# The product of the weights moved ahead of the branch, and the last rows of a two-layer graph kernel rearranged

## The chip, the core and the metric

One core of a Trainium2 chip runs the whole program. Its engines are TensorE (PE, matrix products), VectorE (DVE), ScalarE (ACT), GpSimd (POOL) and SyncE (SP, which here only issues DMAs); ACT and POOL issue DMAs too. The metric is the device time of one execution, in microseconds; less is better. All data are float32.

## What is computed

32 batches of 512 rows by 512 features pass through two graph layers, each with a layer norm ahead of it and the input added behind it:

```
h = max(layernorm(x), 0)
x = x + (adj @ h) @ weight + bias                    # layer 0
h = max(layernorm(x), 0)
q, k, v = h @ Wq + bq, h @ Wk + bk, h @ Wv + bv      # layer 1, 8 heads
scores = q k^T / sqrt(64) + (1 - adj) * -1e9
x = x + (softmax(scores) v) @ Wo + bo
```

`adj` is a 512 by 512 matrix shared by all batches, with values under 1, so in layer 1 the factor -1e9 leaves for each row one neighbour, the one with the largest value, unless two of them are close. The attention then only picks a row of `h`, and layer 1 becomes `h[largest neighbour] @ (Wv Wo) + (bv Wo + bo)`.

## The kernel before

**Ahead of the branch** (lines 68 to 176, `gnn_two_layers`). The kernel loads adj and x of batch 0 in four chunks of 128 rows each, on SP's and ACT's queues, transposes adj on TensorE into `adjT`, normalizes batch 0 into `hs[0]`, and computes that batch's first aggregate, `yT` = (adj h) transposed (line 139, 16 products of 128 by 512, two passes each). Beside it DVE makes the mask (line 115), finds each row's largest neighbour (`top`, `sel`, `idx`), counts the rows that are anyone's neighbour (`used`, line 148, from the small products `few`), and decides whether the shortcut is safe (lines 154 to 167, from `many`); the norms of Wq and Wk enter through ACT's squares. The answer is `flag`, one number that every engine loads (line 178). Then the program branches into `single_path` (taken here, with room for 336 distinct neighbours) or into the general attention.

**Behind the branch** (`single_path`). Each batch needs three large products: `aggregate` (adj h), `layer0` (times the weight) and `layer1` (times `wvo` = Wv Wo, on the rows that are anyone's neighbour only). `product` (line 288) does each in seven pieces on half-size blocks instead of eight, with sums of blocks made by DVE beforehand (`sum_a`, `sum_b`: `h0s`, `adjT_s`, `w0_t`, `yTs` in `sel`, `hTs`, `wvo_t`). Pieces p1, p5, u2, c11, c22, c12, c21 run in that order over three PSUM banks; c22, c12 and c21 add onto a bank that holds an earlier piece, so that piece must first be taken out by `take` (DVE adds or ACT copies). In the last batch's layer0 (line 457) c22 stands ahead of c11.

**The order of the work** is written out by hand. A round `b` has 21 steps, each the length of one piece: steps 0 to 6 under `layer0(b)`, 7 to 13 under `aggregate(b + 1)`, 14 to 20 under `layer1(b - 1)`. `put(batch, step, f)` hangs the work of the other engines on a step; `run` (line 573) emits a piece's products, then the functions of the step, then the piece's take. Each engine runs its own instructions in the order in which they are emitted, so whatever is emitted first also stands first in that engine's queue. Round 0 runs `layer0_rows(0)` and `aggregate(1)`, and in place of a layer 1 `fold_weights` (line 366): it transposes Wv and multiplies it with Wo into `wvo`, and makes `cvo` and `cvo_c`, the bias row and column, from bv, Wo and bo. The loads of Wv and Wo into `xs[3]` and `xs[4]` are the first DMAs behind the branch (line 595). `number_rows` (line 408) gives each used row its place, ten small operations on DVE with two tiny products.

**Rows travel through DRAM.** `put_h` scatters a batch's `h` with indirect DMAs on POOL, so that used rows stand together; `get_h` reads them back (`hc`), `transpose_h` turns them (`hT`); `layer1` writes `zs` (`take_z`); `put_z` transposes and stores it as `z`; `finish` gathers each row's result from `z` by `place` and adds it to `x`; `store` writes the batch out. `look_up` (line 427) fills `place` with four small gathers on POOL, once, in round 1. `zs` has one buffer; its last columns are set to zero by a POOL memset (line 536) that is emitted where `layer1` begins.

**The end.** The last batch, 31, takes its rows by gather from `hs` into `hs[0]` (`get_all`), transposes them (`transpose_all`) and multiplies row chunk by row chunk (`layer1_rows`, line 508). Batches 29 and 30 get their `z` by plain gathers (`fetch`) into `late_z`, and DVE adds them (`add_z`) between the row chunks of batch 31, each followed by its store.

Of the kernel before, what the change touches and what calls it, by code (L numbers as in the profile page):

```python
# [8 lines left out]
F32 = mybir.dt.float32  # L9
# [8 lines left out]
P = 128  # L18
# [7 lines left out]
def gnn_two_layers(ctx: ExitStack, tc: tile.TileContext, x, adj, w0, b0, wq, bq, wk, bk, wv, bv, wo, bo, out):  # L26
# [22 lines left out]
    def big(name):  # L49
# [3 lines left out]
    adjT, yT, w0_s, sel = big("adjT"), big("yT"), big("w0_s"), big("sel")  # L53
    wv_s, wo_s = xs[3], xs[4]
    b0_r = keep.tile([P, D], F32, name="b0_r")
# [7 lines left out]
    kept = dict(xs=xs, hs=hs, adjT=adjT, yT=yT, w0_s=w0_s, sel=sel, wv_s=wv_s, wo_s=wo_s, b0_r=b0_r, used=used,  # L63
                before=before, idx=idx, ident=ident, ones=ones, mhalf=mhalf)
# [3 lines left out]
    with ExitStack() as tmp, tc.manual_schedule():  # L68
# [3 lines left out]
        mask = look.tile([P, C, N], F32, name="mask")  # L72
        for c in range(C):
            nc.sync.dma_start(mask[:, c, :], adj[c * P:(c + 1) * P, :])
            nc.scalar.dma_start(xs[0][:, c, :], x[0, c * P:(c + 1) * P, :])
# [3 lines left out]
        wt = [look.tile([P, DC, D], F32, name=f"wt{i}") for i in range(2)]  # L79
        bt = [look.tile([P, DC], F32, name=f"bt{i}") for i in range(2)]  # L80

        def load_w(t, w):
            nc.scalar.dma_start(t, w.rearrange("(c p) o -> p c o", p=P))

        norms = [Norm(nc, small, mhalf, xs[0], hs[0], [0, 1]), Norm(nc, small, mhalf, xs[0], hs[0], [2, 3])]
        pts = [ps_l.tile([P, C, P], F32, name=f"pt{m}") for m in range(C)]
        for c in range(C):
            for m in range(C):
                nc.tensor.transpose(pts[m][:, c, :], mask[:, c, m * P:(m + 1) * P], ident)
            norms[c // 2].stats(c % 2)  # L90
            if c == 1:
                norms[0].power()
            if c == 2:
                norms[0].offset()
        norms[1].power()
        for t, v in zip(bt, (bq, bk)):
            nc.gpsimd.dma_start(t, v.rearrange("(c p) -> p c", p=P))
        nc.gpsimd.dma_start(b0_r, bass.AP(tensor=b0.tensor, offset=b0.offset, ap=[[0, P], [1, D]]))
        for i, w in enumerate((wq, wk)):
            norms[0].relu(i)  # L100
            load_w(wt[i], w)
        for m in range(C):
            eng = (nc.scalar.copy, nc.scalar.copy, nc.vector.tensor_copy, nc.vector.tensor_copy)[m]
            eng(adjT[:, m, :], pts[m].rearrange("p c q -> p (c q)"))
        norms[1].offset()
        for i in range(2):
            norms[1].relu(i)
        if B > 1:
            load_w(xs[1], x[1])
        load_w(w0_s, w0)  # L110

        sums = look.tile([P, 4], F32, name="sums")
        top = look.tile([P, C, 8], F32, name="top")
        for c in range(C):
            nc.vector.tensor_scalar(mask[:, c, :], mask[:, c, :], 1.0, NEG, op0=ALU.subtract, op1=ALU.mult)
            nc.vector.max(top[:, c, :], mask[:, c, :])
            nc.vector.tensor_scalar(sel[:, c, :], mask[:, c, :], top[:, c, 0:1], None, op0=ALU.is_equal)
        both = look.tile([P, N], F32, name="both")
# [6 lines left out]
        nc.vector.tensor_reduce(least, gap, AX.X, ALU.min)  # L125

        if B > 1:
            norms.append(Norm(nc, small, mhalf, xs[1], hs[1], range(C)))
            norms[2].stats(0)
            norms[2].stats(1)  # L130
        few = ps_l.tile([P, 4, C], F32, name="few")
        many = ps_l.tile([P, 4, C], F32, name="many")
        for d in range(DC):
            ps = ps_l.tile([P, N], F32, name="mm", bufs=2)
            for m in range(C):
                if d == 3 and m == 2:
                    nc.tensor.matmul(many[:, 0, :], ones, used, start=True, stop=True)
                    nc.tensor.matmul(many[:, 1, :], ones, sums, start=True, stop=True)
                nc.tensor.matmul(ps, hs[0][:, m, d * P:(d + 1) * P], adjT[:, m, :], start=(m == 0), stop=(m == C - 1))  # L139
            if d < 2:  # L140
                nc.scalar.activation(bt[d], bt[d], AF.Square, accum_out=sums[:, 2 * d + 1:2 * d + 2])
            nc.scalar.copy(yT[:, d, :], ps)
            if d < 2:
                nc.scalar.activation(wt[d], wt[d], AF.Square, accum_out=sums[:, 2 * d:2 * d + 1])
            if d == 2:
                for m in range(C):
                    nc.tensor.matmul(few[:, 0, m:m + 1], both[:, m * P:(m + 1) * P], ones[:, 0:1], start=True, stop=True)
                nc.vector.tensor_scalar_min(used, few[:, 0, :], 1.0)
                if B > 1:
                    norms[2].stats(2)  # L150
                    norms[2].stats(3)
                    norms[2].power()
        rows = look.tile([P, 1], F32, name="rows")
        nc.vector.tensor_reduce(rows, many[:, 0, :], AX.X, ALU.add)
        fits = look.tile([P, 1], F32, name="fits")
        nc.vector.tensor_scalar(fits, rows, float(ROOM[0]), None, op0=ALU.is_le)
# [798 lines left out]
```

## Time and profile before

| what | us |
|---|---|
| median of 3 runs (lowest, highest) | 1096.13 (1095.85, 1096.92) |
| the profiled execution | 1098.71 |
| its span, first to last instruction | 1097.0 |
| ahead of the branch: first product of the aggregate (line 139) | 10.79 |
| flag written | 29.09 to 29.23 |
| first product behind the branch (line 464) | 30.34 |
| product of the weights, 32 passes (line 378) | 60.36 to 74.26 |
| first piece of layer0(1) | 74.96 |
| last product of TensorE ends | 1087.02 |

A line of the timeline reads: start, duration, engine, line, operation, written tile <- read tiles, shape, count (instructions of one kind in a row are merged), and in brackets the engine's idle time just before with what ended it. The list of waits reads: engine and line that waited <- what released it: total, times, longest. A releaser is inferred from semaphore events and can be missing ("unknown queue"). Ends of matmuls are modelled.

### The profile page before, as it was taken

The page shows a single profiled execution, that of the slowest core. Times are in us where ns is not written, and L with a number is a line of the kernel's source. Part 1 is how long each engine was busy: PE and PEld are TensorE (multiplying, and loading weights), DVE is VectorE, ACT ScalarE, POOL GpSimd, SP SyncE. Part 2 cuts the span into 40 slices and gives each one's busy share as a digit, 9 for nine tenths or more (in the row PEclk, how much of TensorE's full clock was granted, in tenths as well). Part 3 has the DMA queues.
Part 4 walks back from the last instruction along what each step waited for, and adds up shares of the span by engine and source line. Part 5 has one row for each costly group of instructions (what it writes and reads, how often), then busy time and mean ns, then how long its engine had stood idle before and what let it go on. Part 6 is the DMA issues. An engine that isn't in the chain of part 4 may idle for free.

```text
span 1097.0 us, 15882 instructions
## 1 busy us (share of the span) xinstructions
PE 1071.3 (98%) x5404; PEld 941.6 (86%) x5404; DVE 903.2 (82%) x1854; ACT 357.0 (33%) x655; POOL 445.7 (41%) x522
## 2 busy tenths in 40 slices
PE   7999999999999999999999999999999999999996
PEld 3558899999989989989998998999998899999883
DVE  6868888898888889878888888888988888898863
ACT  4223232333223233323233322323332232333221
POOL 1124443335543334544333554443355434345422
PEclk9999999999999999999999999999999999999999
DMA  7362666677676667766667767666777766676547
GB/s 239 125 142 66 156 160 155 185 198 182 180 174 153 159 187 201 180 169 159 163 167 201 184 184 172 152 171 174 202 179 183 171 147 172 183 196 152 147 118 228
DMA packets 162412, 186.90 MB, mean 170 GB/s; under 512 B 14993, under 2 KB 102289, under 8 KB 162321
## 3 DMA queue, kind: packets, MB, share of 16 engines
q1 hardware_dynamic: 130672, 112.70, 37.5%
q0 software_dynamic: 27968, 66.61, 27.0%
q10 hardware_dynamic: 3680, 6.49, 1.7%
q8 instruction: 44, 0.72, 0.3%
q14 instruction: 48, 0.39, 0.1%
HBM read 96.28 MB, written 89.46 MB: 169 GB/s over the span
## 4 chain that ended last, share of the span: by engine, by line
PE 91%; DVE 3%; DMA 2%; POOL 1%; issue 1%; ACT 1%; another core or an unknown queue 0%; SPq 0%; ACTq 0%; POOLq 0%; DVEq 0%
PE mm L294 85%; PE mm L139 2%; PE mm L464 1%; PE mm L378 1%; POOL x L552 1%; PE mm L514 1%; DMA yT<-z,place 1%; DMA x<-in_x_dram 1%; DMA z<-zr 0%; DVE st L199 0%; ACT h L217 0%; DVE zr L543 0%; DVE x L351 0%; DMA hc<-hs 0%
## 5 line engine op out<-in xcount | busy, mean ns | idle before, releaser
L552 POOL DMA_INDIRECT x<-z,place x116 | 182.8, 1576 | 366.3 <-DMA z<-zr 299.4
L333 ACT COPY yT<-mm 128x512 f32<-128x512 f32 x124 | 71.8, 579 | 561.1 <-PE mm L294 487.6
L351 DVE TENSOR_TENSOR x<-mm,x 128x512 f32<-128x512 f32 x217 | 149.7, 690 | 86.1 <-PE mm L294 86.1
L217 ACT ACTIVATE h<-x,off,rstd 128x512 f32<-128x512 f32 x256 | 194.9, 808 | 41.3 <-DVE off L209 40.5
L206 POOL TENSOR_TENSOR rstd<-ve,mhalf 128x2 f32<-128x2 f32 (+1 forms) x97 | 106.5, 1098 | 218.5 <-DVE ve L205 218.3
L199 DVE BATCH_NORM_STATS2 st<-x 128x6 f32<-128x512 f32 x256 | 171.6, 670 | 9.2 <-DMA x<-in_x_dram 8.0
L294 PE MATMUL mm<-w_t,sel 128*128 128x256 f32 x744 | 171.0, 379 | 0.8 <-DVE x L351 0.8
L294 PE MATMUL mm<-adjT_s,h0s 128*128 128x256 f32 x744 | 171.0, 379 | 0.7 <-ACT yT L333 0.7
L294 PEld LDWEIGHTS mm<-w_t,sel 128*128 128x128 f32 x744 | 141.2, 190 | 20.7 <-DVE x L351 1.6
L294 PEld LDWEIGHTS mm<-adjT_s,h0s 128*128 128x128 f32 x744 | 141.1, 190 | 20.7 <-ACT yT L333 1.6
L476 POOL DMA_INDIRECT hs<-h,dest x124 | 133.2, 1075 | 31.2 <-issue 22.2
L294 PE MATMUL mm<-adjT,h 128*128 128x256 f32 x496 | 117.2, 379 | 0.0
L294 PE MATMUL mm<-w_s,yT 128*128 128x256 f32 x496 | 117.2, 379 | 0.0
L294 PE MATMUL mm<-hTs,wvo_t 128*128 128x168 f32 x720 | 113.7, 307 | 3.5 <-ACT zs L344 3.5
L344 ACT ACTIVATE zs<-mm,cvo_c 128x168 f32<-128x168 f32 x248 | 85.6, 397 | 88.6 <-PE mm L294 84.9
L294 PEld LDWEIGHTS mm<-hTs,wvo_t 128*128 128x128 f32 x720 | 106.0, 191 | 4.2 <-ACT zs L344 4.2
L294 PEld LDWEIGHTS mm<-adjT,h 128*128 128x128 f32 x496 | 94.2, 190 | 13.2 <-issue 0.5
L294 PEld LDWEIGHTS mm<-w_s,yT 128*128 128x128 f32 x496 | 92.9, 190 | 11.7 <-issue 0.5
L442 DVE TENSOR_TENSOR x<-x,b_r 128x512 f32<-128x512 f32 x128 | 86.6, 678 | 0.0
L294 PE MATMUL mm<-hT,wvo 128*128 128x168 f32 x480 | 79.4, 309 | 0.0
L294 PEld LDWEIGHTS mm<-hT,wvo 128*128 128x128 f32 x480 | 73.8, 192 | 1.5
L331 DVE TENSOR_TENSOR yT<-mm,yT 128x512 f32<-128x512 f32 x93 | 63.9, 687 | 7.0 <-PE mm L294 3.0
(148 smaller groups left out, 1273.4 us busy)
## 6 DMA issues: line engine op xcount, KB each, us to landing
out_dram<-x SPq DMA_DIRECT2D x124, 256.0 KB
x<-in_x_dram SPq DMA_DIRECT2D x120, 256.0 KB
hc<-hs SPq DMA_DIRECT2D x124, 176.0 KB
z<-zr SPq DMA_DIRECT2D x120, 96.0 KB
z<-zr SPq DMA_DIRECT2D x120, 80.0 KB
hs<-h,dest POOLq DMA_INDIRECT x124, 6.2
x<-z,place POOLq DMA_INDIRECT x116
x<-in_x_dram ACTq DMA_DIRECT2D x4, 256.0 KB
```

The costliest lines, as they stand in the source:

```text
L139: nc.tensor.matmul(ps, hs[0][:, m, d * P:(d + 1) * P], adjT[:, m, :], start=(m == 0), stop=(m == C - 1))
L199: self.nc.vector.bn_stats(st, self.src[:, self.chunks[i], :])
L206: self.nc.gpsimd.tensor_tensor(self.rstd, ve, self.mhalf[:, 0:n], ALU.pow)
L217: self.nc.scalar.activation(dst, src, AF.Relu, bias=self.off[:, i:i + 1], scale=self.rstd[:, i:i + 1])
L294: nc.tensor.matmul(bank[:, m, 0:half], lhs[:, k, m * P:(m + 1) * P], rhs[:, k, :], start=(first and m == 0 and k == 0), stop=(k == 1), ski ...
L331: nc.vector.tensor_add(dst, bank, dst)
L333: nc.scalar.copy(dst, bank)
L344: nc.scalar.activation(dst[:, m, :], bank[:, m, :], AF.Identity, bias=cvo_c[:, 2 * i + m:2 * i + m + 1])
L351: nc.vector.tensor_add(dst, bank, dst)
L442: nc.vector.tensor_add(X[b][:, c, :], X[b][:, c, :], b0_r)
L476: stored = nc.gpsimd.indirect_dma_start(out=HS[b], out_offset=bass.IndirectOffsetOnAxis(ap=dest[:, i:i + 1], axis=0), in_=H1[b][:, i, :], ...
L552: nc.gpsimd.indirect_dma_start(out=X[b][:, c, :], out_offset=None, in_=Z[b], in_offset=bass.IndirectOffsetOnAxis(ap=place[:, c:c + 1], axi ...
```

## The change

Two ends of the program change; rounds 2 to 28 keep their code.

Front: Wv and Wo are loaded first, chunk by chunk on both queues, then adj, x of batch 0, Wq, Wk, w0 and x of batch 1, all on SP. Wv is transposed and multiplied with Wo ahead of the branch; adj is transposed between the four parts of that product, by which ACT instead of DVE makes the mask, in two operations for each chunk. Then comes the aggregate of batch 0. The product for `flag` stands two products ahead of the aggregate's end, the counts a chunk earlier. `cvo`, `cvo_c`, the sums of adjT and the first two of w0, and the addition of b0 to batch 0 are done ahead of the branch. Behind it, `number_rows` moves to step 1, some norms, sums and scatters of round 0 to earlier steps, `look_up` from step 11 to step 16 of round 1; round 0 has no third product any more.

End: the last batch's layer0 has the order of pieces of the others; batch 30's `zs` takes the buffer of `h0s`; two stores of batch 29's `z` go to ACT's queue; the first `transpose_all` is at step 18 of round 31; the row chunk's own addition and store come ahead of the `add_z`, which are spread two to each chunk.

The diff, cut to its core:

```diff
+    adjT, yT, w0_s, sel, wvo = big("adjT"), big("yT"), big("w0_s"), big("sel"), big("wvo")
+    adjT_s, w0_t = (keep.tile([P, 4, 2, N // 2], F32, name=n) for n in ("adjT_s", "w0_t"))
     wv_s, wo_s = xs[3], xs[4]
...
+        wt = [look.tile([P, DC, D], F32, name=f"wt{i}") for i in range(2)]
+        bt = [look.tile([P, DC], F32, name=f"bt{i}") for i in range(2)]
+        bv_c = look.tile([P, DC], F32, name="bv_c")
+        wvT = yT
...
+        for t, w in ((wv_s, wv), (wo_s, wo)):
+            for c in range(DC):
+                (nc.sync, nc.scalar)[c % 2].dma_start(t[:, c:c + 1, :], rows(w, c, 1))
+        for t, w in ((adj_s, adj), (xs[0], x[0])):
+            for c in (0, 2):
+                nc.sync.dma_start(t[:, c:c + 2, :], rows(w, c, 2))
+        for t, w in [(wt[0], wq), (wt[1], wk), (w0_s, w0)] + [(xs[1], x[1])] * (B > 1):
+            nc.sync.dma_start(t, rows(w, 0, C))
         make_identity(nc, ident)
         nc.gpsimd.memset(ones, 1.0)
         nc.gpsimd.memset(mhalf, -0.5)
...
+        for t, v in ((bv_c, bv), (bt[0], bq), (bt[1], bk)):
+            nc.gpsimd.dma_start(t, v.rearrange("(c p) -> p c", p=P))
+        first = look.tile([P, 1], F32, name="first")
+        nc.scalar.activation(first, ones[:, 0:1], AF.Relu)
...
+        for _ in transposed(wv_s, wvT, (nc.scalar.copy, nc.vector.tensor_copy, nc.scalar.copy, nc.vector.tensor_copy)):
+            pass
+        for c in range(C):
+            nc.scalar.activation(mask[:, c, :], adj_s[:, c, :], AF.Copy, bias=-1.0)
+            nc.scalar.activation(mask[:, c, :], mask[:, c, :], AF.Copy, scale=NEG)
...
+        flips = transposed(adj_s, adjT, (nc.scalar.copy,) * 4)
+        for i in range(DC):
+            ps = ps_l.tile([P, D], F32, name="mm", bufs=2)
+            for j in range(DC):
+                nc.tensor.matmul(ps, wvT[:, j, i * P:(i + 1) * P], wo_s[:, j, :], start=(j == 0), stop=(j == DC - 1))
+            if i == 0:
+                next(flips)
+                peaks(0)
+                peaks(1)
+            if i == 1:
+                next(flips)
+                for n in (0, 1):
+                    norms[0].stats(n)
+                norms[0].power()
+                for v, r in ((b0, b0_r), (bo, cvo)):
+                    nc.gpsimd.dma_start(r, bass.AP(tensor=v.tensor, offset=v.offset, ap=[[0, P], [1, D]]))
+                norms[1].stats(0)
+                norms[0].offset()
+                norms[1].stats(1)
+                norms[1].power()
+            nc.scalar.copy(wvo[:, i, :].rearrange("p (c q e) -> p q c e", q=4, c=4),
+                           ps.rearrange("p (q c e) -> p q c e", q=4, c=4))
+            if i == 1:
+                next(flips)
+                norms[0].relu(0)
+                norms[0].relu(1)
+                peaks(2)
+                norms[1].offset()
...
+        for i in range(4):
+            sum_b(nc, adjT_s, adjT, i)
...
         for d in range(DC):
             ps = ps_l.tile([P, N], F32, name="mm", bufs=2)
             for m in range(C):
-                if d == 3 and m == 2:
+                if d == 2 and m == 1:
                     nc.tensor.matmul(many[:, 0, :], ones, used, start=True, stop=True)
                     nc.tensor.matmul(many[:, 1, :], ones, sums, start=True, stop=True)
+                if d == 3 and m == 2:
+                    nc.tensor.matmul(few[0:1, 1, 0:1], sure, ones[:, 0:1], start=True, stop=True)
+                if d == 3 and m == 0:
+                    bias = ps_l.tile([P, D], F32, name="pt0")
+                    nc.tensor.matmul(bias, ones, part, start=True, stop=True)
                 nc.tensor.matmul(ps, hs[0][:, m, d * P:(d + 1) * P], adjT[:, m, :], start=(m == 0), stop=(m == C - 1))
-            if d < 2:
...
-            if d == 2:
+            if d == 0:
+                squares(1)
                 for m in range(C):
                     nc.tensor.matmul(few[:, 0, m:m + 1], both[:, m * P:(m + 1) * P], ones[:, 0:1], start=True, stop=True)
...
+                for i in range(2):
+                    sum_b(nc, w0_t, w0_s, i)
+                if B > 1:
+                    norms[2].offset()
+            if d == 2:
+                decide()
+                nc.vector.memset(before[:, 0:1], 0.0)
+                for m in range(1, C + 1):
+                    nc.vector.tensor_add(before[:, m:m + 1], before[:, m - 1:m], many[:, 0, m - 1:m])
+                for c in (0, 1):
+                    nc.vector.max_index(idx[:, c, :], top[:, c, :], mask[:, c, :])
         nc.vector.tensor_copy(flag, few[0:1, 1, 0:1])
+        for c in (2, 3):
+            nc.vector.max_index(idx[:, c, :], top[:, c, :], mask[:, c, :])
+        nc.vector.tensor_add(cvo, bias, cvo)
+        nc.vector.tensor_mul(part.rearrange("p (c q e) -> p c q e", q=4, c=4),
+                             cvo.rearrange("p (q c e) -> p c q e", q=4, c=4),
+                             ident.rearrange("p (q e) -> p q e", q=4).unsqueeze(1).broadcast_to([P, 4, 4, 32]))
+        nc.vector.tensor_reduce(cvo_c, part.rearrange("p (c n) -> p c n", c=DC), AX.X, ALU.add)
         if B > 1:
-            norms[2].offset()
             for c in range(C):
                 norms[2].relu(c)
-        nc.vector.memset(before[:, 0:1], 0.0)
-        for m in range(1, C + 1):
-            nc.vector.tensor_add(before[:, m:m + 1], before[:, m - 1:m], many[:, 0, m - 1:m])
-        for c in range(C):
-            nc.vector.max_index(idx[:, c, :], top[:, c, :], mask[:, c, :])
+        for c in range(C):
+            nc.vector.tensor_add(xs[0][:, c, :], xs[0][:, c, :], b0_r)
 
...
     def layer0(b):
-        if b == B - 1:
-            return product(yT, yTs, w0_s, w0_t, take_onto(X[b]), pieces=("p1", "p5", "u2", "c22", "c11", "c12", "c21"))
...
-            for bz, c in ((), ((B - 3, 0), (B - 3, 1)), ((B - 3, 2), (B - 3, 3)), [(B - 2, c) for c in range(C)])[r]:
-                add_z(bz, c, nc.sync if bz == B - 3 else nc.scalar)
             x_r = X[b][:, r, :].rearrange("p (q c e) -> p q c e", q=4, c=4)
             nc.vector.tensor_add(x_r, bank.rearrange("p (c q e) -> p q c e", q=4, c=4), x_r)
             nc.sync.dma_start(out[b, r * P:(r + 1) * P, :], X[b][:, r, :])
+            for i in range(2):
+                add_z(B - 3 + r // 2, 2 * (r % 2) + i, nc.sync if r < 2 else nc.scalar)
...
-        ZT[b] = work.tile([P, DC, 32 * S], F32, name="zs")
+        ZT[b] = work.tile([P, DC, 32 * S], F32, name="h0s" if b == B - 2 else "zs")
...
-            eng = nc.scalar if b == B - 2 and s0 == 0 and q > 1 else nc.sync
+            eng = nc.scalar if q > 1 and (b, s0) in ((B - 3, 6), (B - 2, 0)) else nc.sync
...
-        for t, w in ((wv_s, wv), (wo_s, wo)):
-            nc.sync.dma_start(t, w.rearrange("(c p) o -> p c o", p=P))
-        nc.gpsimd.dma_start(bv_c, bv.rearrange("(c p) -> p c", p=P))
-        nc.gpsimd.dma_start(cvo, bass.AP(tensor=bo.tensor, offset=bo.offset, ap=[[0, P], [1, D]]))
...
-                put(b + 2, 2, load_x)
+                put(b + 2, 2 * b, load_x)
...
-            put(b, 9 if b > 0 else 15, put_h, 0)
...
+            put(b, 9, put_h, 0)
...
-            for step, i in ((13, 0), (13, 1), (13, 2), (14, 3)) if b == B - 2 else \
-                    ((14, 0), (15, 1), (16, 2), (18, 3)) if b > 0 else ((14, 0), (16, 1), (17, 2), (18, 3)):
+            for i, step in enumerate((13, 13, 13, 14) if b in (0, B - 2) else (14, 15, 16, 18)):
...
+            if b == 0:
+                put(0, 1, lambda b: number_rows())
+                for i in (2, 3):
+                    put(0, 12, lambda b, i: sum_b(nc, w0_t, w0_s, i), i)
...
+            if b == B - 1:
+                put(b, 18, lambda b: transpose_all(0))
...
-                put(1, 11, lambda b: look_up(tables[0]))
-                for step, i in ((4, 0), (4, 1), (5, 2), (5, 3)):
+                put(1, 16, lambda b: look_up(tables[0]))
...
-            if b == 0:
-                for step, c in ((0, 0), (0, 1), (1, 2), (2, 3)):
...
-                for step, i in ((0, 0), (0, 1), (1, 2), (1, 3)):
-                    put(0, step, lambda b, i: sum_b(adjT_s, adjT, i), i)
...
-                put(0, 11, lambda b: number_rows())
-                for step, i in ((11, 0), (12, 1), (12, 2), (13, 3)):
...
-                for j in range(DC):
-                    put(0, 16 + j, lambda b, j: bias_part(j), j)
...
             run(aggregate(b + 1) if b + 1 < B else layer1(b - 2) if b < B else None, todo[7:14])
-            if b == 0:
-                run(fold_weights(), todo[14:21])
-            else:
-                run(layer1(b - 1) if b < B and b != B - 2 else None, todo[14:21])
+            run(layer1(b - 1) if 0 < b < B and b != B - 2 else None, todo[14:21])
```

## Prediction

> **What bounds the kernel now.** I read the page first (busy shares, then the chain that ended last), then TensorE's own waits, then its timeline at the front, at 100 us and at the end, and last what DVE, ACT and POOL do in those places.
>
> ```profile
> PE 1071.3 (98%) x5404; PEld 941.6 (86%) x5404; DVE 903.2 (82%) x1854; ACT 357.0 (33%) x655; POOL 445.7 (41%) x522
> PE 91%; DVE 3%; DMA 2%; POOL 1%; issue 1%; ACT 1%; another core or an unknown queue 0%; SPq 0%; ACTq 0%; POOLq 0%; DVEq 0%
> ```
>
> TensorE is busy for 98% of the span and is 91% of the chain, nearly all of it line 294, the seven-piece products. The change leaves those products alone, so a gain can only come from time in which TensorE stands still, or runs slowly. The list of its waits is short:
>
> ```profile
> PE pt L89 <- DMA mask<-in_adj_dram: 5.2, 3, 4.8
> PE mm L294 <- ACT zs L344: 3.5, 2, 2.7
> PE mm L464 <- ACT h L217: 1.3, 1, 1.3
> PE mm L294 <- DVE yT L331: 1.1, 1, 1.1
> PE mm L139 <- ACT adjT L104: 1.1, 1, 1.1
> PE mm L294 <- issue: 0.9, 1, 0.9
> PE mm L514 <- ACT h L503: 0.8, 1, 0.8
> PE mm L294 <- DVE x L351: 0.8, 1, 0.8
> ```
>
> Its timeline says where they are: at the front, once at 101.8 us, and in the last 60 us.
>
> ```profile
> 4.76 2.27 PE L89 MATMUL pt<-ident,mask 128*128 128x128 f32 x8 [4.76 <-DMA mask<-in_adj_dram]
> 10.79 13.36 PE L139 MATMUL mm<-adjT,h 128*128 128x512 f32 x24 [1.07 <-ACT adjT L104]
> 56.22 1.99 PE L294 MATMUL mm<-adjT_s,h 128*128 128x256 f32 x8 [1.10 <-DVE yT L331]
> 60.36 13.90 PE L378 MATMUL mm<-x,zs 128*128 128x512 f32 x32
> 104.49 1.95 PE L294 MATMUL mm<-hTs,wvo_t 128*128 128x168 f32 x8 [2.67 <-ACT zs L344]
> 106.23 2.45 PE L294 MATMUL mm<-hT,wvo 128*128 128x168 f32 x8
> 1045.03 1.99 PE L294 MATMUL mm<-w_t,sel 128*128 128x256 f32 x8 [0.79 <-DVE x L351]
> 1064.43 1.41 PE L294 MATMUL mm<-adjT_s,wvo_t 128*128 128x168 f32 x8 [0.92 <-issue]
> 1071.70 1.98 PE L514 MATMUL mm<-wvo,h 128*128 128x512 f32 x4 [0.82 <-ACT h L503]
> ```
>
> See that until 10.79 us TensorE has done nothing but 16 transposes, while the product of the weights (60.36, 13.90 us) is done later, when it is the bound. Between 109 and 1013 us the table of stages shows it busy throughout but for one idle 0.7 us.
>
> **What the Trainium skill says.** "TensorE: Matmul & The Clock Gate", Part 1, says the array runs at half rate until it has been busy for a free-running window of about 3.4 us, and goes back after an idle one. The trace agrees: 24 passes took 13.36 us where 24 x 0.429 = 10.3 would do, and after the idle 2.67 us the pieces at 104 and 106 us took 1.95 and 2.45 instead of 1.30. Part 4 there says that transposes don't count as busy for this gate; the trace agrees, since after 16 transposes the products at 10.79 were still slow. "DMA: Bandwidth & Descriptors", Issuing engines are not separate DMA queues, says that loads issued by several engines share the same 16 engines; here 2 MB on two queues moved at 395 to 402 GB/s (4 to 8 us), later loads on ACT's queue alone at 228 to 408.
>
> **The change, part by part**, against the profiled execution (1098.71 us, span 1097.0; the median of the runs is 1096.13, 2.58 lower).
>
> *Front.* The wv chunks take the places of the adj and x chunks in the queues, so the first lands at about 4.8 us as these did. Sixteen transposes at 2.27/8 each end at 9.3; the first copy (0.6) is done by then since its last transpose is the first of the last four. wo's chunks follow at 7.3 to 8.7, as the later adj and x chunks did. So 32 product passes start at 9.3, not the aggregate at 10.79: -1.5. The adj transposes move into the fast stream, 16 x 0.13 = +2.1 (the weights' own run there now at 1.04 per 8); the weights' transposes leave it (58.05 to 60.36), -2.3. The slow clock is met once as before, by one stream instead of the other: 0, +-0.9 for where the window falls.
>
> What must keep up: adj (next 1 MB, at 350 GB/s by 12) is wanted at 16, x0 (by 15) at 24 by ACT's norms. ACT's list up to the aggregate is 2 copies, 8 mask operations (nearest row 0.81, about 0.7 in a chain: 5.7 us, 11.5 to 17.5), wvo copies of 0.59, 4 adjT copies after TensorE's last adj transposes (21.7 to 24), 4 norms of 0.73 with a wvo copy between, to 27.3. TensorE ends the product at 9.3 + 13.7 + 2.5 (slow clock) + 2.1 = 27.6, and wants the last chunk of h 1.7 us later. Hidden, with 2 us to spare. POOL's loads of bv, bq and bk now come first, 1.18 and 0.81 to issue as before, where POOL is idle until 7.4; at 6.9 to landing bv is there by 9, for the bias part. The early activation takes the table load (1.28, at 4.87 before) out of the way of the first copy: 0, as ACT was idle. DVE (copies, bias part 2.7, four peaks of 1.2, four norm statistics of 0.9, sums) is done by 27. The aggregate with its small products ends at 43.4.
>
> *Flag.* Before, flag was written at 29.23, after TensorE's last product, and it restarted at 30.34; idle from about 28.8, 1.5 us. Now the small product for it stands two products (four passes) before the end, so flag is written about 1.5 us before TensorE ends, and the load and branch (0.9 us) are covered. What is late next: the first bank after the branch was the bias sum's, which DVE reads after flag and two index searches (2 x 0.75): about 44.2, 0.7 to 0.8 after the end. -0.8; ends 0 and -1.2. The b0 additions (4 x 0.6) now stand on DVE ahead of the branch, and the row takes wait behind them to 48.7; six banks cover that.
>
> *First batch.* number_rows moves from step 11 to step 1: its ten small DVE operations (53.3 to 55.0) no longer delay the yT take: -1.1. Folding's bias product (2 passes) only moves. layer0(1) follows aggregate(1) directly; its sums are emitted at step 13, as for the batch 31 before, where the trace shows no gap (1037.17 to 1042). The norms of the first rounds come some steps earlier, cvo and the sums of adjT and w0 ahead of the branch, the weights' loads are gone from SP behind it, so x2 comes sooner: the same instructions beside a busy TensorE, 0. Steps 14 to 20 of the first round, spread under the folding before, now follow in one go; DVE has one yT sum (0.7) there. So layer0(1) starts at 74.96 - 1.5 - 0.2 - 0.8 - 1.1 = 71.4: **-3.6**, ends -2.3 and -4.9.
>
> *Places.* At 101.8 TensorE waits for ACT's first zs take, and ACT for something the trace calls an unknown queue, until 103.7. Just then, once in the run, POOL issues four place gathers (97.38 to 102.38) ahead of zs's memset, beside SP's hc loads. They go to step 16, behind the memset and the rstd. I take the wait as theirs: 2.67 idle, and the slow clock after it, 111.97 - 104.49 = 7.48 us for five pieces of 1.14, 1.78 lost: **-4.45**. The other end is 0: the trace doesn't show that the gathers are the cause. Behind them at step 16 POOL has only finish(0), at 119 us, with 15 us idle ahead.
>
> *End.* Plain order of pieces in the last layer0: c11 stands between u2 and c22 again, so the bank is taken in time: -1.05 (13.14 us from 1038.90 to 1052.04 against 7 x 1.726). zs of batch 30 in h0s's buffer removes ACT's wait for DVE's transposes of batch 29's zs (0.92). But two z stores of batch 29 now go out on ACT's queue, 0.85 for two, ahead of ACT's c21 take: p1's take ends about 3.1 us after the product starts, wanted at 2.3. So that stall stays: 0. First transposes of the last rows at step 18, as their gather (1062.6 + 4.6) lands: -0.82. TensorE ends 1.9 earlier. Behind it, gather and add of batch 30's z: last gather landed at 1090.5, then the row add, queued behind it on DVE, 0.6, then a store. The z stores and gathers move with TensorE by 1.05; the row add now stands ahead of the last two z adds: 1.05 + 0.6, and out stores of batch 29 start one row earlier, freeing DMA (share 1.00 at 1075 to 1080): **-2.4**, ends -1 and -3.5.
>
> Sum: -3.6 - 4.45 - 2.4 = -10.45, so 1098.71 becomes 1088.3. The profiled run lies above the others by 2.58; I do not know how much of the one-off stall the others have, so I keep 1088 as the forecast for the median too, a gain of 8.
>
> **Rivals.**
> - *The stall at 101.8 isn't the gathers'*, or is not in ordinary runs. For: the trace names no queue, memset's columns don't overlap the takes. Against: nothing else is peculiar to that place. Then 1096.13 - 6.0 = 1090.1.
> - *ACT takes over at the front.* It now has masks, copies and norms in one file; if the norms end 3.6 us after 27.6 the front's gain is gone, and the stall may stay too: about 1093.7. For: they queue behind four copies. Against: ACT is 33% busy, slack 2 us.
> - *Slower: x1 late.* All eight MB follow on SP's queue, x1 last, and DVE's statistics of x1 stand ahead of `used`, which TensorE wants at about 36 for the counts. Landing after 35 costs TensorE a us for each us, and from 43 on, a mean of 190 GB/s after the first 2 MB, more than the whole gain; at 46 us of landing, with the clock slowed again, 1099. Against: 228 to 408 GB/s puts it at 24 to 32.
>
> **How the numbers follow.** Forecast 0.45, stall stays 0.28, ACT 0.13, slower 0.14. The first two hold 1083.3 (all far ends) to 1092.8 (all near ends); with half of the third the range is 1083.3 to 1093.8. Within 0.2% (2.2 us, about what can be told from no change) falls half of the ACT case: faster 0.79, same 0.07, slower 0.14.
>
> **What would show it.** First product at about 9.3 us, layer0_rows at 44, layer0(1) at 71.4, no wait on DVE's yT; no idle TensorE at about 98, no second slow stretch of the clock; in the last 60 us the waits on DVE x and ACT h gone, the two on ACT's zs left; the last DVE operation a z add. Wrong: TensorE waiting on `used` or on h near 28 to 36 us, or a new wait within the first two batches.

## The result: 1084.9 us, and the profile after

| | before | after |
|---|---|---|
| median (lowest to highest) | 1096.53 (1095.85 to 1097.96), 4 runs | 1084.90 (1083.45 to 1085.40), 4 runs |
| ratio, 95% interval | | 0.989 (0.9873 to 0.9907) |
| the profiled execution; its span | 1098.71; 1097.0 | 1083.45; 1081.3 |
| first piece of layer0(1) | 74.96 | 67.65 |
| layer0(1) to layer0(2) | 37.01 | 33.24 |
| layer0(2) to layer0(31) | 926.93 | 926.46 |
| layer0(31) to TensorE's last product | 48.12 | 45.65 |
| from there to the end of the span | 9.97 | 8.33 |

The change gains 11.6 us; 8 was forecast, with 1083.3 to 1093.8 as the range. TensorE's list of waits in the kernel after (total, times, longest):

```profile
PE pt L106 <- DMA x<-in_L_gnn_Wv_dram: 4.7, 1, 4.7
PE mm L364 <- ACT zs L414: 1.4, 2, 0.8
PE mm L364 <- DVE zs L411: 0.8, 1, 0.8
PE mm L491 <- ACT yT L209: 0.7, 1, 0.7
PE mm L364 <- ACT yT L403: 0.3, 1, 0.3
PE mm L364 <- issue: 0.3, 1, 0.3
```

The waits on DVE's yT, on DVE's x and on ACT's h are gone; of the ones on ACT's zs, two are left where there were three (3.5 us of two and the 0.92 shown as issue). One is new, on DVE's zs. TensorE's timeline after says where:

```profile
4.66 3.57 PE L106 MATMUL pt<-ident,x 128*128 128x128 f32 x16 [4.66 <-DMA x<-in_L_gnn_Wv_dram]
8.35 3.94 PE L134 MATMUL mm<-x,yT 128*128 128x512 f32 x8
...
13.00 3.60 PE L134 MATMUL mm<-x,yT 128*128 128x512 f32 x8
...
41.31 7.11 PE L491 MATMUL mm<-w_s,yT 128*128 128x512 f32 x16 [0.72 <-ACT yT L209]
...
67.65 1.89 PE L364 MATMUL mm<-w_s,yT 128*128 128x256 f32 x8
...
99.65 1.41 PE L364 MATMUL mm<-hTs,wvo 128*128 128x168 f32 x8 [0.82 <-DVE zs L411]
...
1051.54 1.41 PE L364 MATMUL mm<-adjT_s,wvo_t 128*128 128x168 f32 x8 [0.64 <-ACT zs L414]
...
1067.68 5.32 PE L541 MATMUL mm<-wvo,h 128*128 128x512 f32 x12
```

See the first three lines. Sixteen transposes stand back to back, 0.22 us each; the eight product passes behind them take 3.94 us where eight at full rate (third line) take 3.60. So the clock is full almost from the first product; the trace's own record of the clock puts the step (the moment at which it becomes full) at 8.03 us. In the kernel before, 24 passes took 13.36 us instead of 10.3, and the step came at 16.46. Near 100 us there is no wait of 2.7 us and no second slow stretch. The last operations of DVE after:

```profile
1074.46 0.68 DVE L543 TENSOR_TENSOR x<-mm,x 128x512 f32<-128x512 f32 x1
1075.07 0.68 DVE L593 TENSOR_TENSOR x<-yT,x 128x512 f32<-128x512 f32 x1
1076.38 0.69 DVE L593 TENSOR_TENSOR x<-yT,x 128x512 f32<-128x512 f32 x1 [0.63 <-DMA yT<-z,place]
```

The last row's own addition (line 543) is no longer last: the end waits for the gather of batch 30's z (1076.38).

One pair of profiles is not enough to split the gain, for two reasons that the runs below showed. The step of the clock is not tied to the program: in the traces' record every stretch of full or slow clock behind the first step, but for the last at the program's end, is a whole number of windows of 3.413 us (26, 1 and 288 in before, 28, 2 and 287 in `b_fill`, 313 in after), but the first step came at 13.96 to 16.61 us in four kernels with the front of before, and at 8.03 to 9.82 in six with the front of after. With it the first piece of layer0(1) ranged from 73.58 to 75.06 us in the four and from 67.65 to 68.48 in the six. And the chips differ: the kernel before took 1092.9 and 1092.7 us (medians) on one chip, 1096.7 and 1097.0 on two others.

### The profile page after: what moved, and what is told of

The parts are those of the page before. It is cut to its first block, busy times and chain, and to the rows that moved or that the text cites. A ratio compares the mean times of both kernels' runs of the same rounds, so it can differ in the third digit from the quotient of the medians.

```text
span 1081.3 us, 15886 instructions
## 1 busy us (share of the span) xinstructions
PE 1064.6 (98%) x5404; PEld 939.3 (87%) x5404; DVE 902.7 (83%) x1850; ACT 362.1 (33%) x664; POOL 441.9 (41%) x522
## 4 chain that ended last, share of the span: by engine, by line
PE 92%; DVE 3%; DMA 1%; POOL 1%; issue 1%; ACT 1%; SPq 0%; ACTq 0%; DVEq 0%; POOLq 0%
PE mm L364 87%; PE mm L134 1%; PE mm L206 1%; PE mm L491 1%; PE mm L541 1%; DVE st L284 1%; DMA yT<-z,place 1%; POOL x L579 1%; PE pt L106 0%; DVE x L421 0%; DMA x<-in_L_gnn_Wv_dram 0%; DVE x L471 0%; DMA hc<-hs 0%; ACT h L302 0%; DMA z<-zr 0%
## 5 line engine op out<-in xcount | busy, mean ns | idle before, releaser
L503 POOL DMA_INDIRECT hs<-h,dest x124 | 128.6, 1037 | 23.8 <-issue 22.4
L414 ACT ACTIVATE zs<-mm,cvo_c 128x168 f32<-128x168 f32 x240 | 83.1, 398 | 77.3 <-PE mm L364 73.4
L471 DVE TENSOR_TENSOR x<-x,b_r 128x512 f32<-128x512 f32 x124 | 83.8, 676 | 0.0
```

The lines of the kernel that those rows point to most:

```text
L414: nc.scalar.activation(dst[:, m, :], bank[:, m, :], AF.Identity, bias=cvo_c[:, 2 * i + m:2 * i + m + 1])
L471: nc.vector.tensor_add(X[b][:, c, :], X[b][:, c, :], b0_r)
L503: stored = nc.gpsimd.indirect_dma_start(out=HS[b], out_offset=bass.IndirectOffsetOnAxis(ap=dest[:, i:i + 1], axis=0), in_=H1[b][:, i, :], ...
```

## The experiments

Ratios are to the kernel before on the same chip; "1093 chip" and "1097 chip" say what that one took there.

**The place gathers.** `b_places16` is the kernel before with one edit:

```diff
-                put(1, 11, lambda b: look_up(tables[0]))
+                put(1, 16, lambda b: look_up(tables[0]))
```

> The kernel before with one edit: the four place gathers stand at step 16 of round 1 instead of step 11. Theory (the wait of 2.67 us at 101.8 us and the slow clock behind it are caused by these gathers): the wait is gone from TensorE's list, the clock stays full from 16.5 us to the last us, the stretch from layer0(1) to layer0(2) falls from 37.0 to about 32.5 us, and the median falls by 4.0 to 4.5 us (ratio about 0.996). Rival (the wait belongs to something else in that place, or only to the one profiled execution): the median moves by less than 0.5 us (ratio 0.9995 to 1.0005).

On a 1093 chip: 1092.63 us, ratio 0.9998 (0.9989 to 1.0006). No gain; but on that chip two kernels with the gathers still at step 11 (`b_end` and `b_warm`, below) have no stall either: layer0(1) to layer0(2) takes 32.92 and 32.91 us in them. There was nothing to remove. Once more, on another chip:

> Once more the kernel before with the place gathers at step 16 instead of step 11, for the case that the chip is one on which the kernel before takes 1095 to 1099 us and has the stall (on a chip where before takes 1093 it had none and the edit changed nothing). Gathers as the cause of the stall, on such a chip: the wait of 2.7 us and the second slow stretch of the clock are gone, the stretch from layer0(1) to layer0(2) is 32.9 us instead of 37 to 38.4, and the time falls by 3.5 to 5 us (ratio 0.9955 to 0.997). Something else that holds ACT there, with ACT's own instructions unchanged: ratio 0.9995 to 1.0005 and the wait stays. On a chip without the stall this run tells nothing new.

On a 1097 chip: 1093.99 us, ratio 0.9974 (0.9964 to 0.9985), a gain of 3.0 us. TensorE's timeline of this run, at the place of the stall:

```profile
98.00 1.30 PE L294 MATMUL mm<-hT,wvo 128*128 128x168 f32 x8
99.14 2.44 PE L294 MATMUL mm<-hTs,wvo_t 128*128 128x168 f32 x16
101.42 1.30 PE L294 MATMUL mm<-hT,wvo 128*128 128x168 f32 x8
```

The second and third piece (x16) run through. On the other 1097 chip, `b_fill` (below), which leaves the gathers at step 11, has the stall as the first profile had it. TensorE's timeline, then ACT's:

```profile
99.83 1.30 PE L302 MATMUL mm<-hTs,wvo_t 128*128 128x168 f32 x8
103.91 2.61 PE L302 MATMUL mm<-hTs,wvo_t 128*128 128x168 f32 x8 [2.78 <-ACT zs L352]
```

```profile
100.17 0.59 ACT L341 COPY yT<-mm 128x512 f32<-128x512 f32 x1 [6.18 <-PE mm L302]
103.17 1.28 ACT L352 ACTIVATE zs<-mm,cvo_c 128x168 f32<-128x168 f32 x4 [2.41 <-remote]
```

ACT stands idle for 2.41 us in front of a take whose piece had been done since 100 us, while POOL issues the fourth gather (100.67 to 101.69). In `b_warm`, on the 1093 chip, POOL issues the same four gathers at 97.64 to 102.64, and ACT doesn't wait for them:

```profile
101.03 0.69 ACT L347 ACTIVATE zs<-mm,cvo_c 128x168 f32<-128x168 f32 x2 [0.62 <-PE mm L297]
```

So with the gathers at step 11 the wait is in the traces of before and of `b_fill` and in none of the 1093 chip, and on a chip where before takes 1097, moving them gains 3.0 us. By what path they hold ACT, no trace shows ("remote"). The edit also brings zs's memset ahead of the gathers (95.71 us in `b_places16_2`, 102.38 in before), and no run tells the two apart; but in `b_warm` the take begins ahead of the memset (102.64), so the program doesn't make ACT wait for that one. Nor is the wait in every execution: one of the 31 of the kernel before on these two chips (1093.64 us, with a mean clock of 0.999 where the others have 0.994 to 0.997) looks free of it. Does the kernel after need the move as well?

```diff
-                put(1, 16, lambda b: look_up(tables[0]))
+                put(1, 11, lambda b: look_up(tables[0]))
```

> The kernel after with one edit: the four place gathers back at step 11 of round 1. Theory (the gathers there hold up the first take of zs): a wait on ACT zs of 2 to 3 us appears near 95 us, with a second slow stretch of the clock, and the time rises by 4.0 to 4.5 us over that of the kernel after, to about 1089. Rival (the gathers are not the cause): no such wait, and the time is that of the kernel after, 1084.9, within 0.6 us.

> Once more the kernel after with the place gathers back at step 11 of round 1, for the case that the chip is one on which the kernel before takes 1095 to 1099 us. If the gathers at step 11 hold up the first take of zs on such chips whatever else the program does: a wait of 2 to 3 us on ACT zs near 95 us, slow clock behind it, stretch from layer0(1) to layer0(2) 36 to 38 us instead of 33.2, median 1088 to 1090 us. If the rest of the change has taken away what the gathers collided with: 1084.5 to 1086 us and no such wait. On a chip where before takes 1093 it tells nothing new.

Both fell on the 1093 chip: 1085.44 (0.9935, 0.9921 to 0.9948) and 1084.06 us (0.9918, 0.9904 to 0.9931), no wait. For a 1097 chip this stays open. What they do show is the gain of the rest of the change where there is no stall to remove: 7.5 and 8.6 us.

**The kernel after, unchanged, on a 1097 chip** (`a_copy`).

> The kernel after, unchanged, beside the others of this call. If the gain lies in the work the change moves and not in the stall at 101.8 us of the one profiled execution of before: its time is that seen so far, 1084 to 1086 us, a gain of 7 to 8 us where before takes 1093, and of 11 to 12 where before takes 1096.5. If the gathers' stall is part of before in ordinary runs too: 11 to 12 us whatever the absolute times.

1085.30 us, ratio 0.9902 (0.9887 to 0.9917): a gain of 11.4. The kernel after takes 1084.9 and 1085.3 us where before takes 1096.5 and 1096.7, and on the 1093 chip the two runs above, which differ from it by the gathers alone, take much the same. Of the 4 us by which the kernel before differs between chips, moving the gathers takes away 3.0. One of the six executions here took 1088.5 us with a mean clock of 0.995 (0.997 to 0.998 in the others); what slowed it, no trace shows.

**The clock at the front.** `b_warm`: the kernel before, with

```diff
+        warm = ps_l.tile([P, N], F32, name="mm", bufs=2)
+        for _ in range(7):
+            nc.tensor.matmul(warm[:, 0:P], ones, ones, start=True, stop=True)
```

ahead of the first transposes.

> The kernel before with seven more products of 128 by 128 (of a tile of ones by itself, into a bank that nobody reads: only work is added) ahead of TensorE's first transposes, while it waits for adj. Theory (transposes count for the clock, a window of 3.4 us full of work makes it full, and in the kernel before the transposes with gaps between 4.8 and 10 us fell short of it): with about 3 us of products in front the clock is full by 11 us instead of 16.5, and the median falls by 1.5 to 2.9 us (ratio 0.9973 to 0.9986). Rival (transposes don't count, so the work between 4.8 and 10.8 us leaves the array cold whatever came before): the clock is full at some time before 8 us, falls back, and is full again only behind 14 us; the median moves by less than 0.5 us.

1093.14 us, ratio 1.0002 (0.9994 to 1.001). TensorE's timeline of the profiled execution:

```profile
1.59 3.35 PE L81 MATMUL mm<-ones 128*128 128x128 f32 x14 [1.59 <-POOL mhalf L78]
5.57 3.55 PE L92 MATMUL pt<-ident,mask 128*128 128x128 f32 x12 [0.62 <-DMA mask<-in_adj_dram]
9.31 1.11 PE L92 MATMUL pt<-ident,mask 128*128 128x128 f32 x4 [0.19 <-DMA mask<-in_adj_dram]
11.68 12.72 PE L142 MATMUL mm<-adjT,h 128*128 128x512 f32 x24 [1.26 <-ACT adjT L107]
```

The clock is full at 16.06 us. It looks like the rival, but there are gaps: from one start to the next these instructions take 0.21 us, and so counted there are 0.3 to 0.4 us between the four groups of transposes. Of the windows of 3.41 us counted back from 16.06, only the last was full. The one from 5.8 to 9.2 holds twelve transposes, 2.6 us at 0.21 each, about three quarters (the profile, which models the ends, has 3.12 us busy); that from 9.2 to 12.6 is 2.03 us busy. In nine of the thirteen executions the mean clock was 0.994 to 0.996 and not 0.998 as in the profiled one, so the clock may have gone another way there; no trace of these is kept. The run doesn't settle the question, and `b_fill` fills the gaps too:

```diff
...
+        fill(8)
...
             for m in range(C):
                 nc.tensor.transpose(pts[m][:, c, :], mask[:, c, m * P:(m + 1) * P], ident)
+            fill((1, 1, 2, 4)[c])
```

> The kernel before with products of ones by ones (into a bank that nobody reads: only work is added) in every gap of TensorE's first 11 us: eight ahead of the first transposes, one or two between the chunks, four between the last transposes and the aggregate. The run with seven in front alone left gaps of 0.2 to 1.3 us and changed neither clock nor time. Theory (the clock becomes full after one window of 3.4 us with hardly a gap in it, transposes counted): full by 5.0 to 8.5 us instead of 15.3 to 16.6, the first 24 passes of the aggregate take 10.3 to 10.8 us instead of 12.7 to 13.4; DVE's statistics of x1, which wait for a load until 22.9 us, then stand ahead of the counts, so that about 1 us of it is given back: the median falls by 1.5 to 2.6 us (ratio 0.9976 to 0.9986). Rival (transposes don't count): full only after about 14 us, ratio 1.000 to 1.0005.

```profile
6.45 1.06 PE L96 MATMUL pt<-ident,mask 128*128 128x128 f32 x4
7.30 0.54 PE L83 MATMUL mm<-ones 128*128 128x128 f32 x2
7.68 0.60 PE L96 MATMUL pt<-ident,mask 128*128 128x128 f32 x4
...
11.09 7.13 PE L147 MATMUL mm<-adjT,h 128*128 128x512 f32 x16 [1.03 <-ACT adjT L112]
18.57 3.70 PE L147 MATMUL mm<-adjT,h 128*128 128x512 f32 x8 [0.34 <-ACT yT L150]
...
25.20 0.39 PE L145 MATMUL many<-used,ones 128*128 128x4 f32 x2 [0.32 <-DVE used L156]
...
28.16 0.19 PE L174 MATMUL few<-ones,sure 128*1 128x1 f32 x2 [0.53 <-DVE sure L173]
```

This is TensorE's timeline of `b_fill` (`fill(n)`, whose definition is left out above, emits n of those products). The clock is full at 7.63 us: four transposes take 0.60 us there, 1.06 just before. Half of the work in the 3.41 us ahead of that was transposes. The 24 passes take 7.13 + 3.70 us and not 13.4. And yet the time is 1096.85 us, ratio 0.9997 (0.9988 to 1.0007): the gain expected of it did not come. The last lines say why. TensorE now waits for ACT's yT, for `used` and for `sure`; the last two stand on DVE behind the statistics of x1, whose load lands at 23.4 us. layer0(1) starts at 74.27 us, 0.2 ahead of the mean of the four fronts of before.

That doesn't make the slow clock free in the old front. With the step at 13.96 (`b_places16_2`) and at 16.61 (`b_places16`) the 24 passes take 12.26 and 13.42 us and start 0.31 apart, and layer0(1) starts at 73.58 and 75.06: there the whole difference arrives. What `b_fill` shows is how soon that ends, because x1 is late next. The other way round, `a_split` breaks up the transposes of the kernel after, by putting all of Wv on one queue:

```diff
-                (nc.sync, nc.scalar)[c % 2].dma_start(t[:, c:c + 1, :], rows(w, c, 1))
+                (nc.sync, nc.scalar)[t is wo_s].dma_start(t[:, c:c + 1, :], rows(w, c, 1))
```

> The kernel after with one edit: all of Wv's chunks on SP's queue and all of Wo's on ACT's, as adj and x were in the kernel before, so that Wv lands chunk by chunk and its transposes have gaps. Theory (the clock needs a window of work with hardly a gap, and half of the front's gain is that Wv's transposes stand back to back): transposes 4.8 to 9.5 us, first product at about 9.6 (+1.3), clock full only 3.4 to 6.8 us later, at 13 to 16.5, the first products slow for that long: first piece of layer0(1) at about 71 to 72.5 instead of 67.7 to 68.0, and the time 3 to 4.5 us over the kernel after in the same call. Rival (the clock follows the products and transposes don't count): as in after the products follow one another, +1.3 us for the later start and no more.

TensorE's timeline of `a_split`, then the first product in `a_copy`:

```profile
7.63 1.11 PE L106 MATMUL pt<-ident,x 128*128 128x128 f32 x4 [0.55 <-DMA x<-in_L_gnn_Wv_dram]
10.48 1.12 PE L106 MATMUL pt<-ident,x 128*128 128x128 f32 x4 [1.74 <-DMA x<-in_L_gnn_Wv_dram]
11.63 4.96 PE L134 MATMUL mm<-x,yT 128*128 128x512 f32 x8
```

```profile
8.42 4.70 PE L134 MATMUL mm<-x,yT 128*128 128x512 f32 x8
```

1089.63 us, 4.3 more than `a_copy` on the same chip, and layer0(1) at 71.96. The size is in the range expected, its parts are not: the last chunk came so late that the product starts 3.2 us later than in `a_copy` (8.42), and the clock, full at 14.22 instead of 9.82, adds only 0.26 us to the first eight passes (4.96 against 4.70). The rest is 1.0 us in round 1, where the wait on DVE's zs grew to 1.8. So here it is the landing of Wv that counts, and the clock is the smaller part; as the edit moved both, it doesn't test the gaps alone.

**The end.** `b_end` is the kernel before with every edit of the end and none of the others:

```diff
-        if b == B - 1:
-            return product(yT, yTs, w0_s, w0_t, take_onto(X[b]), pieces=("p1", "p5", "u2", "c22", "c11", "c12", "c21"))
...
+        ZT[b] = work.tile([P, DC, 32 * S], F32, name="h0s" if b == B - 2 else "zs")
...
+            eng = nc.scalar if q > 1 and (b, s0) in ((B - 3, 6), (B - 2, 0)) else nc.sync
...
+                add_z(B - 3 + r // 2, 2 * (r % 2) + i, nc.sync if r < 2 else nc.scalar)
...
+                put(b, 18, lambda b: transpose_all(0))
```

> The kernel before with all the edits of the end and none of the others: plain order of pieces in the last layer0, zs of batch 30 in the buffer of h0s, two z stores of batch 29 on ACT, first transposes of the last rows at step 18, row addition ahead of the z additions. Reading of the two traces: the end is worth 4.1 us, median about 1092.4 (ratio 0.9962), last layer0 12.09 us, tail behind TensorE's last product 8.3 us. The prediction's sum: 2.4 us, median about 1094.1 (ratio 0.9978). If the first of these is due to the state of the end alone, the span from the first piece of the last layer0 to the end is 54.0 us as in the kernel after; by the second it is 55.7.

1091.04 us, ratio 0.9981 (0.9975 to 0.9988): 1.3 to 2.7 us. The prediction's 2.4 lies within. The 4.1 us of the first pair of profiles was too much: there the tail of before, 9.97 us, was the longest of all kernels with its end (8.2 to 9.3 in the others), and that of after, 8.33, the shortest with the new one (8.4 to 9.4). Next, `a_zSP` puts two stores of batch 29's z back on SP in the kernel after:

```diff
-            eng = nc.scalar if q > 1 and (b, s0) in ((B - 3, 6), (B - 2, 0)) else nc.sync
+            eng = nc.scalar if b == B - 2 and s0 == 0 and q > 1 else nc.sync
```

> The kernel after with the two z stores of batch 29 that went to ACT's queue back on SP's. The prediction's step (these stores stand ahead of ACT's c21 take and so keep the stall before batch 30's second piece): the wait of 0.64 to 1.2 us on ACT's zs near 1051.5 us goes, TensorE ends 0.6 to 0.9 us earlier, and the time falls by 0 to 0.9 us, less if the z stores on one queue land later. Rival (the stall is the take's own wait for its bank, not the stores'): the wait stays as it is and the time moves by less than 0.3 us or rises.

TensorE's timeline, then DVE's last operation:

```profile
1050.35 2.44 PE L364 MATMUL mm<-adjT_s,wvo_t 128*128 128x168 f32 x16
```

```profile
1077.28 0.69 DVE L593 TENSOR_TENSOR x<-yT,x 128x512 f32<-128x512 f32 x1 [0.33 <-DMA yT<-z,place]
```

The wait before batch 30's second piece is gone (x16 without a bracket), and TensorE's part of the end is 44.74 us instead of 45.65. But the tail grows to 10.46 us, for the last z addition still waits for its gather, and the time is 1085.07, beside 1084.9 and 1085.3 for the kernel after on other chips. So the stores on ACT's queue do cause that wait, as the prediction had it, and removing it gained nothing that can be seen: the end is set by the way of z. Last, `a_adds_old`, the kernel after with the old order of the additions:

```diff
+            for bz, c in ((), ((B - 3, 0), (B - 3, 1)), ((B - 3, 2), (B - 3, 3)), [(B - 2, c) for c in range(C)])[r]:
+                add_z(bz, c, nc.sync if bz == B - 3 else nc.scalar)
             x_r = X[b][:, r, :].rearrange("p (q c e) -> p q c e", q=4, c=4)
...
-            for i in range(2):
-                add_z(B - 3 + r // 2, 2 * (r % 2) + i, nc.sync if r < 2 else nc.scalar)
```

> The kernel after with the order of the last additions as before: no z addition in the first row chunk, two in the second and third, four ahead of the last row's own addition. The prediction's step (the row addition stood behind the last z additions and costs one addition of 0.6 us, and the out stores of batch 29 start a row later): TensorE's end unchanged, tail behind its last product 0.6 to 1.5 us longer than 8.3 to 9.0, the time 0.5 to 1.5 us over the kernel after. Rival (the tail is set by the landing of z's gathers alone): within 0.3 us of the kernel after, and the last operation of DVE ends at the same distance from the last gather's landing but for 0.6 us.

```profile
1078.27 0.69 DVE L593 TENSOR_TENSOR x<-yT,x 128x512 f32<-128x512 f32 x1 [0.79 <-DMA yT<-z,place]
1078.88 0.69 DVE L545 TENSOR_TENSOR x<-mm,x 128x512 f32<-128x512 f32 x1
```

1086.81 us, ratio 0.9941 (0.9928 to 0.9955), beside 0.9918 and 0.9935 for the two runs of `a_places11`, with after's end, on the same chip. TensorE's part is the same 45.65 us, the tail 10.58. DVE's last lines show one part of it: the row addition stands behind the z addition, 0.6 us. The stretch behind the last addition, with a row's store on SP's queue instead of a z's on ACT's, takes 5.1 us, as in all five kernels with the old end; it took 4.3 in six of the eight with the new end, but 5.8 and 5.3 in the other two (`a_copy`, `a_zSP`), and why isn't shown. Whether the gathers land later too can't be told: the last z addition begins 4.2 us after TensorE's last product here, and 1.9 to 4.5 us after it in those eight.

**The new wait.** `a_wvo0`: the kernel after with DVE's four sums for `wvo_t` a round earlier.

```diff
+                for i, step in enumerate((0, 0, 13, 13)):
+                    put(0, step, lambda b, i: sum_a(wvo_t, wvo, i), i)
...
-                for i, step in enumerate((5, 5, 6, 6)):
-                    put(1, step, lambda b, i: sum_a(wvo_t, wvo, i), i)
```

> The kernel after with the four sums wvo_t moved from steps 5 and 6 of round 1 to steps 0 and 13 of round 0, where DVE has idle time (1.8 us at 47 to 48.8). Theory (the 0.8 us wait on DVE's zs near 99.7 us, new in the kernel after, is DVE's backlog in round 1): the wait falls to 0.3 us or nothing, stretch from layer0(1) to layer0(2) 32.4 to 32.9 us instead of 33.24, time 0.3 to 0.8 us under after. Rival (the wait is set by the order of DVE's queue near step 15, behind POOL's rstd): the wait stays at 0.8 us and the time is the same within 0.3 us.

The wait before the last piece of layer1(0), on DVE's zs, falls from 0.82 to 0.27 us, so DVE's backlog in round 1 is its cause; but the sums now delay a take of x, TensorE waits 0.89 us at 72.98, and the time is 1085.13 us against 1085.30 for `a_copy`. No experiment was faster than the kernel after by more than its interval.

## Why the prediction was right, and where it wasn't

Mean of the profiles of each front or end, against the prediction's terms:

| term | predicted | measured |
|---|---|---|
| front | -3.6 | -6.4 (74.5 to 68.1, four profiles and six) |
| places | -4.45, other end 0 | 1097 chips: -3.0; 1093 chip: 0 |
| new wait on DVE's zs | none | +0.3 (32.9 to 33.2) |
| end | -2.4 | -2.1 (ratio of `b_end`) |
| outside the span | none | +0.4 (1.7 to 2.1 us) |

The last row is the time of an execution less its span. `a_wvo0`, with the same front, has 1.8 us there, so what makes it 2.1 is open. With -0.3 in the rounds between, they make -11.1 on a 1097 chip, where 11.6 and 11.4 were measured.

- **Front.** The size was off, in two terms. "Sixteen transposes at 2.27/8 each end at 9.3": the row of before from which 2.27 was read holds gaps, as adj came in chunk by chunk. Without gaps sixteen take 3.57 us, and the product starts at 8.35: 0.9 us. And "the slow clock is met once as before, by one stream instead of the other: 0": the prediction took from the Trainium skill ("TensorE: Matmul & The Clock Gate", Part 4) that transposes don't count as busy, and said that the trace agreed. It didn't test that: before, the transposes had gaps, and with such gaps the clock did not become full in `b_warm` either. After, they have none, and the clock is full at 8.03 us, when TensorE had done nothing but transposes; so too in `a_places11_2` (transposes until 8.61 us, step at 8.47). Here the measurement decides against the page. The first eight passes lose 0.3 to 1.1 us to the clock and no longer the 2.0 to 3.1 of 24 passes before: some 2 us. With 0.9 that is the missing 2.8. The sum is worked out from the traces of both fronts, and no run has the new front with the clock alone held back. What supports it is that the clock's part arrives whole in the new front: in `a_copy` the first eight passes take 0.76 us longer than in after (4.70 against 3.94) and start 0.07 later, and layer0(1) starts 0.83 later. There the operands are in time: x1 lands at 27.9 us and the counts are wanted at 33. In the old front, `b_fill` gained 0.2 us by a clock that was full still earlier.
- **Flag and number_rows** were right: a gap of 0.72 us at layer0_rows (0.7 to 0.8 predicted), though what ends it is ACT's copy of yT and not the bank; the wait on DVE's yT is gone. ACT and x1, the bases of two rivals, were in time.
- **Places.** The mechanism was right for such a chip as the forecast was made on, and the size a little too large: 3.0 in the medians instead of 4.45, which was read from one execution (in the profiles the stretch from layer0(1) to layer0(2) went from 37.01 to 32.92). The rival, that ordinary runs don't have the stall, is true of the 1093 chip. The prediction could not see that a profile of one chip doesn't speak for all.
- **End.** Right in sum and in its parts: -1.05 for the pieces; the stall kept by ACT's stores; the first row's wait for transposes gone; the row addition out of the tail.

So the sum of the terms, 10.45, came near the measured 11.6 partly by luck: the front was 2.8 too small, the places 1.45 too large. The forecast of 8 was lower because it took off the 2.58 by which the profiled execution lay above the median, not knowing whether ordinary runs have the stall; on the 1097 chips they do.

## What to carry to other kernels

Before pricing a clock or a stall, ask what is late next: a clock full from 7.63 us gave some 2 us of TensorE's time and nothing of the kernel's in the old front, where x1 was late next, and 0.9 us of TensorE's time saved at the end gave nothing either. Price an operation from a row without gaps: a mean over a group that waited holds the wait. And before believing a one-off stall of a profile, compare the spread of ordinary runs on more than one chip.

## What the runs showed that had not been expected

- Transposes back to back for one window of 3.41 us (4.62 to 8.03) are enough to make the clock full; in `b_warm` a window with transposes for about three quarters of it (0.21 us each) was not.
- The time of a kernel can depend on the chip in one place: four small gathers cost 3 us on one chip, their stall is in the trace of a second (medians 1097.0 and 1096.7 for the kernel before), and on a third they cost nothing (1092.9 and 1092.7).
